# A selective-scan kernel with one more slot between its scans and what GpSimd and TensorE do with them

## The chip, the cores and the metric

The kernel runs on one core of one Trainium2 chip. The metric is the device time of one execution in microseconds. Before the change the median of three runs was 6442.46 us (6440.53 to 6453.84). Engines are called as in the profile: PE is TensorE's matmul, PEld its weight load, DVE is VectorE, ACT is ScalarE, POOL is GpSimd, and SP is the engine whose queue issues all DMAs of this kernel.

## The reference

Four layers work on `x` of shape (4, 96, 64, 64) in float32. The change touches the scan of layer 0 alone; layer 1 is a convolution block, layer 2 a spectral block with a small feed-forward network, layer 3 linear attention with another.

```python
# layer 0, for each of the 4 images; L = 4096, 192 channels d, 16 states n, 4 directions k
u     = silu(depthwise_conv(Win @ group_norm(x)))
xs    = [u, u^T, flip(u), flip(u^T)]                  # one sequence for each direction
dts, Bs, Cs = split(sel_w @ xs)
delta = softplus(dt_w @ dts + dt_b)
h     = h * exp(delta * A) + (delta * u) * B          # along L, for every (d, n)
y     = sum over n of h * C                           # + Ds * xs
out   = Wout @ layer_norm(y0 + y1 + y2 + y3)
```

So each of 4 images x 4 directions x 192 channels x 16 states is a recurrence over 4096 positions, followed by a product with C and a sum over the 16 states.

## The kernel before, in words

**Units and slots.** A sequence is cut into 8 chunks of 512 positions (`NCH`, `CH`). An image, a direction and a chunk make a *step*: 4 x 4 x 8 = 128 steps. A step is cut into 12 *units* (`u` = 0 to 11). A unit holds 64 channels (`i`) and 4 states (`j`) as two halves `e` of 128 partitions x 512 positions, so there are 1536 units. `PASSES` runs units 0 to 7 over `j` with `i` = 0 and 1 in turn, then units 8 to 11 over `j` with `i` = 2.

The loop at the end of `scans` has one *slot* for each unit. `manual_schedule` keeps every engine's instructions in the order in which this loop writes them; each engine, the DMA queue of SP too, works through its own list in order, and semaphores hold it where data or a buffer is missing. In slot s the loop writes, in this order:

- loads for the next step (`LOADS`, `fetch`) and the stores owed from the slot before (`flush`), both on SP;
- `decays(s + 1)`: on ACT, the two exponentials of the next unit into two PSUM banks `ps_da` (a ring of four banks, so two units). Before them `keep(s - 1)` copies the last column of the unit before into `state`, from which the next step's scan starts: two 128x1 copies on ACT, or one 128x2 copy on POOL where POOL makes the unit's product;
- `product(s - 1)`: on POOL, h times C, in place in the result tile `hc` (128x1024). Only the units of `POOL_C` have this, five of twelve;
- `inputs(s + 2)`: on POOL, the tile `db` = (delta u) B of the unit two slots ahead (128x1024), from a ring of three;
- `states(s)`: on DVE, two `tensor_tensor_scan` instructions. For the other seven units DVE also makes the two products with C, into `hc`;
- `sums`: on PE, for a pair of units, four matmuls with `const("stack")` into the single PSUM bank `ps_y`. The pair (s - 3, s - 2) is summed in slot s, since `when = at + 2` with `at` the odd unit. After the last pair of a pass ACT copies the bank to `yt`, and two stores to DRAM follow in the next slot;
- `advance`: work of all other layers, cut into small PE, ACT and DVE pieces (`Stage`), fills the slot up to a share of each engine. Its loads and stores go through the same SP queue.

**Buffers.** `SCAN` gives the rings: 3 tiles each for `rep_d` and `rep_g` (delta and delta u, repeated over partitions), 5 for `rep_BC` (rows of B and C, repeated), 3 for `db` and 5 for `hc`. A step uses four `rep_BC` tiles, `BC` 0 to 3, one for each `j`. A load into a tile waits until the last reader of its former content is done. `BC` 3 is loaded in slot 12 (`PC`), which is slot 0 of the step that uses it, and is first read by `inputs` of unit 6, in slot 4.

**Other work that hangs on the scans.** `through` counts finished steps in `scanned[b]`. The stages `turn` and `scan_outputs`, which add the four directions up, look at this count before they issue their loads. When the scans are over, the remaining stages of the last image are written without slots (`force`).

The lines of the profile: L1274 `inputs`, L1284 the exponentials, L1293 the scans, L1298 DVE's product with C, L1308 and L1310 the state copies, L1313 `product`, L1334 `sums`, L1345 the copy to `yt`, L1243 and L1249 the loads of `rep_BC` and of `rep_g` and `rep_d`, L444 the stores in `flush`.

Of the kernel before, what the change touches and what calls it, by code (L numbers as in the profile page):

```python
# [40 lines left out]

KORDER = [(0, 1, 3, 2)] * (B - 1) + [(1, 3, 0, 2)]

SCAN = {"rep_d": 3, "rep_g": 3, "rep_BC": 5, "db": 3, "hc": 5}
POOL_C = (1, 3, 6, 8, 10)
LAST = {"tab": 24, "more": 6}
TMP, IN = 10, 5

PC = NI * NJ // 2
# [46 lines left out]
def hybrid_kernel(ctx: ExitStack, tc: tile.TileContext, a: dict):  # L96
# [10 lines left out]
    pool = lambda name, bufs=1, **kw: ctx.enter_context(tc.tile_pool(name=name, bufs=bufs, **kw))  # L107
# [13 lines left out]
    def bank(tag="mm", turn=True):  # L121

        if alone and tag == "mm" and turn:
            tag = turns(alone)
        if tag == "mm":
            held_banks[0] += 1
        return psum.tile([128, CH], F32, name=f"ps_{tag}", tag=tag, bufs=BANKS[tag])
# [14 lines left out]
    def const(name, rows=slice(0, 128)):  # L142
        return cst[rows, CS[name]]
# [45 lines left out]
    def pair(tag):  # L189
        return sp.tile([128, 2, CH], F32, name=tag, tag=tag, bufs=SCAN[tag])  # L190

# [245 lines left out]
    def later(out, t, then=None):  # L437

        to_store.append((out, t, then))

    def flush():
        while to_store:
            out, t, then = to_store.pop(0)
            store(out, t)  # L444
            if then is not None:
                then()
# [753 lines left out]
    scanned = [0] * B  # L1200
# [15 lines left out]
    def scans(stages):  # L1216
# [12 lines left out]
        units = []  # L1229
        for number, step in enumerate(steps):  # L1230
            step["at"] = number % (K * NCH)
            u = 0
            for which, chans in enumerate(PASSES):
                for j in range(NJ):
                    for i in chans:
                        units.append({"step": step, "number": number, "u": u, "j": j, "i": i, "pass": which,
                                      "pool": u in POOL_C})
                        u += 1

        def load_states(step, j):  # L1240
            t = pair("rep_BC")
            of = d_bc[step["k"]][step["b"] % 3][step["c"], 8 * j : 8 * j + 8].rearrange("(s e) l -> s (e l)", e=2)
            load(t.rearrange("p e l -> p (e l)"), of.unsqueeze(0).to_broadcast([32, 4, 2 * CH]))  # L1243
            step["BC"][j] = t

        def load_channels(step, i, name):
            t = pair(f"rep_{name}")
            of = (d_delta if name == "d" else d_du)[step["k"]][step["b"] % 3][step["c"], 64 * i : 64 * i + 64]
            load(t.rearrange("p e l -> p (e l)"),  # L1249
                 of.rearrange("(p e) l -> p (e l)", e=2).unsqueeze(1).to_broadcast([32, 4, 2 * CH]))  # L1250
            step[name][i] = t

        def need(step):

            while (step["k"] % 2, step["c"]) not in traced[step["b"]]:
                force(stages)
            flush()


        LOADS = {4: [("BC", 0)], 5: [("g", 0)], 6: [("g", 1), ("d", 0)], 7: [("d", 1)], 10: [("BC", 1), ("g", 2)],  # L1260
                 11: [("BC", 2), ("d", 2)], PC: [("BC", 3)]}

        def fetch(step, what):
            for name, i in what:
                if name == "BC":
                    load_states(step, i)
                else:
                    load_channels(step, i, name)
# [3 lines left out]
        def inputs(x):  # L1272
            x["db"] = pair("db")
            nc.gpsimd.tensor_mul(x["db"], x["step"]["g"][x["i"]], both(x["step"]["BC"][x["j"]][:, 0]))  # L1274

        def decays(x, last):
            x["da"] = []
            for e in (0, 1):

                if last is not None:  # L1280
                    keep(last, e)
                av = (x["step"]["k"] * NI + 2 * x["i"] + e) * NJ + x["j"]
                x["da"].append(bank("da"))
                act(x["da"][e], x["step"]["d"][x["i"]][:, e], AF.Exp, scale=aneg[:, av : av + 1])  # L1284
# [15 lines left out]
        def keep(x, e):  # L1300
            step, u = x["step"], x["u"]
            if step["n"] < NCH - 1:
                if "last" not in step:
                    step["last"] = sp.tile([128, NI * NJ], F32, name="state")
                end = 0 if step["k"] >= 2 else CH - 1
                to = step["last"][:, 2 * u : 2 * u + 2]
                if not x["pool"]:
                    nc.scalar.copy(to[:, e : e + 1], x["h"][e][:, end : end + 1])  # L1308
                elif e == 0:
                    nc.gpsimd.tensor_copy(to, x["hc"][:, :, end])  # L1310

        def product(x):
            x["made"] = nc.gpsimd.tensor_mul(x["hc"], x["hc"], both(x["step"]["BC"][x["j"]][:, 1]))  # L1313

        due = {}
        for at in range(1, len(units), 2):
            group = units[at - 1 : at + 1]
            when = at + 2  # L1320
            due.setdefault(when, []).append(group)

        def sums(group):
            step, first, last = group[0]["step"], group[0]["j"] == 0, group[1]["j"] == NJ - 1
            if first:
                step["y"] = bank("y")
            y = step["y"]

            made = None
            for m in (1, 0):  # L1330
                x = group[m]
                for e in (1, 0):
                    q = 2 * m + e
                    done = mm(y[32 * q : 32 * q + 32], lhsT=const("stack"), rhs=x["hc"][:, e],  # L1334
                              start=first or (x["pass"] == 0 and x["j"] == 0), stop=last or (x["pass"] == 0 and x["j"] == NJ - 1))
                    if made is None:
                        made = group[0]["made"]
                        tc.add_manual_dep(done.ins, made.ins.name, mybir.DependencyInfo(
                            mybir.DependencyClass.Sync, mybir.DependencyReason.DATA), reason="sums")
            def through():  # L1340
                scanned[step["b"]] += 1

            if last:
                yt = sp.tile([128, CH], F32, name="yt")
                nc.scalar.copy(yt, y)  # L1345
                to = d_y[step["k"]][step["b"] % 2][step["c"]]
                for m in (0, 1):
                    at = 128 * group[0]["pass"] + 64 * m
                    later(to[at : at + 64].rearrange("(p e) l -> e p l", e=2), yt[64 * m : 64 * m + 64],
                          through if group[0]["pass"] == 1 and m == 1 else None)  # L1350

        owed = 0.0
        stages += plan()
# [5 lines left out]
        inputs(units[0])  # L1359
        inputs(units[1])  # L1360
        decays(units[0], None)
        for slot in range(len(units) + 6):
            clock[0] = slot
            x = units[slot] if slot < len(units) else None
            if x is not None:
                if x["u"] == 0:


                    last = len(units) - NCH * PC
                    if slot < last:  # L1370
                        rate = max(RATE, sum(s.work for s in stages if s not in behind) / (last - slot))
                    else:
                        rate = sum(s.work for s in stages) / (len(units) - slot)
                    if x["number"] > 0:
                        fetch(x["step"], LOADS[PC])
                if x["number"] + 1 < len(steps) and x["u"] in LOADS:
                    if x["u"] == 4:
                        need(steps[x["number"] + 1])
                    fetch(steps[x["number"] + 1], LOADS[x["u"]])
            flush()  # L1380
            if slot + 1 < len(units):
                decays(units[slot + 1], units[slot - 1] if slot > 0 else None)
            if 0 < slot <= len(units):
                if units[slot - 1]["pool"]:
                    product(units[slot - 1])
            if slot + 2 < len(units):
                inputs(units[slot + 2])
            if x is not None:
                states(x)
            for group in due.get(slot, ()):  # L1390
                sums(group)
            for e, (us, most) in SHARE.items():
                room[e] = min(room[e] + us, most)
            tensor[0] = 0.0
            held_banks[0] -= freed[0]
            freed[0] = 0
            owed = min(owed + rate, 8.0)
            while owed > 0.0:
                did = advance(stages)
                if did is None:  # L1400
                    break
                owed -= did
# [241 lines left out]
```

## Time and profile before

| what | value |
|---|---|
| median of 3 runs | 6442.46 us (6440.53 to 6453.84) |
| the profiled execution | 6432.73 us, of it 6430.9 us span on the core |
| granted TensorE clock, mean | 0.836 |
| busy: DVE | 5504.2 us (86%), 6059 instructions |
| busy: POOL | 5176.0 us (80%), 2743 instructions |
| busy: PE | 4759.6 us (74%), 27804 instructions |
| busy: ACT | 4172.2 us (65%), 8040 instructions |
| DMA | 1111.98 MB, 173 GB/s over the span |
| first scan begins, last scan ends | 89.6 us, 6015.9 us |
| mean length of a slot | 5926.3 us / 1536 = 3.86 us |

The durations and waits shown come from this one execution, which was 9.7 us shorter than the median. A busy share over the whole span mixes three parts: 90 us of preparation, 5926 us of slots, and 415 us after the last scan, in which POOL does nothing and PE is busy for 379.1 us. An engine's waits are read from the records of the instruction that starts after an idle time, with the semaphore that ended it.

### The profile page before, as it was taken

The page shows a single profiled execution, that of the slowest core. Times are in us where ns is not written, and L with a number is a line of the kernel's source. Part 1 is how long each engine was busy: PE and PEld are TensorE (multiplying, and loading weights), DVE is VectorE, ACT ScalarE, POOL GpSimd, SP SyncE. Part 2 cuts the span into 40 slices and gives each one's busy share as a digit, 9 for nine tenths or more (in the row PEclk, how much of TensorE's full clock was granted, in tenths as well). Part 3 has the DMA queues.
Part 4 walks back from the last instruction along what each step waited for, and adds up shares of the span by engine and source line. Part 5 has one row for each costly group of instructions (what it writes and reads, how often), then busy time and mean ns, then how long its engine had stood idle before and what let it go on. Part 6 is the DMA issues. An engine that isn't in the chain of part 4 may idle for free. (4 is left out here: it accounts for less than half of the span.)

```text
span 6430.9 us, 84514 instructions
## 1 busy us (share of the span) xinstructions
PE 4759.6 (74%) x27804; PEld 1744.9 (27%) x27804; DVE 5504.2 (86%) x6059; ACT 4172.2 (65%) x8040; POOL 5176.0 (80%) x2743
## 2 busy tenths in 40 slices
PE   7633867757987776786588877667987776857998
PEld 2100212111223621221122254211223531112374
DVE  5979998998999889999899998978999789898345
ACT  5743777865665677887466667856666577665435
POOL 4757878789999889987899988978999789899200
PEclk9755978878998877896799988888998787878999
DMA  5644565676544544466664455465644554555201
GB/s 190 207 155 140 192 208 189 203 236 230 190 152 162 175 164 150 159 201 209 238 216 162 149 183 180 153 215 186 183 155 157 176 173 168 197 189 177 96 10 41
DMA packets 434362, 1111.98 MB, mean 173 GB/s; under 512 B 72474, under 2 KB 74240, under 8 KB 432772
## 3 DMA queue, kind: packets, MB, share of 16 engines
q1 hardware_dynamic: 433924, 1106.58, 51.8%
q8 instruction: 221, 3.62, 0.2%
q14 instruction: 217, 1.78, 0.1%
HBM read 873.41 MB, written 237.44 MB: 173 GB/s over the span
## 5 line engine op out<-in xcount | busy, mean ns | idle before, releaser
L1274 POOL TENSOR_TENSOR db<-rep_g,rep_BC 128x1024 f32<-128x1024 f32 x1536 | 3597.5, 2364 | 344.3 <-DVE ps_da L1293 230.2
L1284 ACT ACTIVATE ps_da<-rep_d,aneg 128x512 f32<-128x512 f32 x3072 | 2062.5, 690 | 438.4 <-DVE hc L1293 320.8
L1293 DVE TENSOR_TENSOR_SCAN ps_da<-ps_da,state,db 128x512 f32<-128x512 f32 x1568 | 1923.2, 1271 | 312.5 <-ACT state L1308 201.3
L1313 POOL TENSOR_TENSOR hc<-hc,rep_BC 128x1024 f32<-128x1024 f32 x640 | 1511.8, 2362 | 112.5 <-DVE hc L1293 58.8
L1334 PE MATMUL ps_y<-hc,cst 128*32 128x512 f32 x6144 | 1018.5, 741 | 627.4 <-POOL hc L1313 352.1
L1293 DVE TENSOR_TENSOR_SCAN hc<-ps_da,state,db 128x512 f32<-128x512 f32 x1120 | 1370.9, 1265 | 107.2 <-issue 43.9
L1298 DVE TENSOR_TENSOR hc<-ps_da,rep_BC 128x512 f32<-128x512 f32 x1792 | 1134.5, 674 | 0.1
L1308 ACT COPY state<-ps_da 128x1 f32<-128x1 f32 x1568 | 247.1, 158 | 499.0 <-DVE hc L1298 498.0
L1334 PEld LDWEIGHTS ps_y<-hc,cst 128*32 128x32 f32 x6144 | 144.7, 118 | 1265.4 <-POOL hc L1313 735.2
L1310 POOL COPY state<-hc 128x2 f32<-128x2 f32 x560 | 106.1, 189 | 369.3 <-DVE hc L1293 341.7
L818 PE MATMUL ps_mm<-h,wd 128*32 128x512 f32 x3192 | 367.1, 595 | 8.3 <-ACT r L155 8.3
L552 PE MATMUL ps_mm<-xp,taps 128*128 128x512 f32 x576 | 295.3, 655 | 52.3 <-ACT ua L554 20.6
L1293 DVE TENSOR_TENSOR_SCAN ps_da<-ps_da,db 128x512 f32<-128x512 f32 x224 | 261.1, 1210 | 51.0 <-ACT state L1308 29.5
L795 PE MATMUL ps_mm<-wd,w 128*32 128x512 f32 x2016 | 256.2, 624 | 32.2 <-DMA wd<-x 20.2
L1345 ACT COPY yt<-ps_y 128x512 f32<-128x512 f32 x256 | 149.2, 583 | 165.1 <-PE ps_y L1334 163.2
L603 PE MATMUL ps_mm<-xd,dtw 128*128 128x512 f32 x256 | 167.0, 745 | 98.4 <-ACT z L625 52.4
L877 PE MATMUL ps_mm<-r,cst 128*128 128x512 f32 x214 | 148.5, 783 | 62.8 <-ACT r L874 18.2
L1293 DVE TENSOR_TENSOR_SCAN hc<-ps_da,db 128x512 f32<-128x512 f32 x160 | 186.0, 1202 | 6.8 <-POOL db L1274 3.0
L799 ACT ACTIVATE h<-ps_mm 128x512 f32<-128x512 f32 x265 | 152.9, 598 | 58.9 <-PE ps_mm L795 57.1
L990 PE MATMUL ps_mm<-wa,xp 128*64 128x96 f32 x1728 | 136.8, 319 | 72.5 <-DVE d L995 61.1
L618 DVE SCALAR_TENSOR_TENSOR ps_mm<-ps_mm,z 128x512 f32<-128x512 f32 x192 | 131.6, 686 | 58.1 <-ACT z L616 54.8
L552 PEld LDWEIGHTS ps_mm<-xp,taps 128*128 128x128 f32 x576 | 115.1, 207 | 228.7 <-issue 159.5
(341 smaller groups left out, 6802.4 us busy)
## 6 DMA issues: line engine op xcount, KB each, us to landing
rep_BC<-bc SPq DMA_DIRECT2D x512, 512.0 KB
rep_g<-du SPq DMA_DIRECT2D x384, 512.0 KB
rep_d<-delta SPq DMA_DIRECT2D x384, 512.0 KB
y<-yt SPq DMA_DIRECT2D x512, 128.0 KB
du<-g SPq DMA_DIRECT2D x128, 256.0 KB
delta<-z SPq DMA_DIRECT2D x128, 256.0 KB
tab<-in_etab SPq DMA_DIRECT2D x112, 256.0 KB
ypart<-y SPq DMA_DIRECT2D x72, 256.0 KB
```

The costliest lines, as they stand in the source:

```text
L552: mm(p, lhsT=taps[:, t, 0:128], rhs=window(t, c + e), start=t == 0, stop=t == 8)
L603: mm(p, lhsT=dtw[:, o + 2 * part, 0:128], rhs=xd, start=True, stop=True)
L795: mm(p[32 * n : 32 * n + 32], lhsT=w1[:, 32 * g : 32 * g + 32], rhs=xin[:, n : n + 15 : 2, 1 : W + 1], start=True, stop=True)
L799: act(h[:, :, 1 : W + 1], split(p), AF.Relu)
L818: mm(p[32 * n : 32 * n + 32], lhsT=held["wd"][:, groups[i], o, dx, :], rhs=here[i][:, :, dx : dx + W], start=dx == 0, stop=dx == 2)
L1274: nc.gpsimd.tensor_mul(x["db"], x["step"]["g"][x["i"]], both(x["step"]["BC"][x["j"]][:, 0]))
L1284: act(x["da"][e], x["step"]["d"][x["i"]][:, e], AF.Exp, scale=aneg[:, av : av + 1])
L1293: nc.vector.tensor_tensor_scan(x["h"][e][:, order], x["da"][e][:, order], x["db"][:, e, order], start, ALU.mult, ALU.add)
L1298: x["made"] = nc.vector.tensor_mul(x["hc"][:, e], x["h"][e], x["step"]["BC"][x["j"]][:, 1])
L1308: nc.scalar.copy(to[:, e : e + 1], x["h"][e][:, end : end + 1])
L1313: x["made"] = nc.gpsimd.tensor_mul(x["hc"], x["hc"], both(x["step"]["BC"][x["j"]][:, 1]))
L1334: done = mm(y[32 * q : 32 * q + 32], lhsT=const("stack"), rhs=x["hc"][:, e], start=first or (x["pass"] == 0 and x["j"] == 0), stop=last or ...
```

## The change

It moves three things later by whole slots, changes two rings and the set of units that POOL multiplies.

- `product` is written for unit s - 2 instead of s - 1, and after `inputs(s + 2)` instead of ahead of it. The state copy of POOL's units moves with it, out of `decays` into `product`.
- `sums` of a pair come two slots later (`at + 4`). The copy to `yt` and its two stores no longer follow the matmuls directly: `sums_out` writes the copy in the slot after, behind that slot's exponentials. `through` is then called with the later stores.
- `db` has 4 tiles instead of 3, `hc` 7 instead of 5.
- `POOL_C` is (1, 3, 5, 7, 10) instead of (1, 3, 6, 8, 10): still five of twelve.
- `BC` 3 is loaded in slot 13, which is slot 1 of its own step.

The number of instructions on PE, DVE, ACT and POOL stays the same; their order changes.

```diff
-SCAN = {"rep_d": 3, "rep_g": 3, "rep_BC": 5, "db": 3, "hc": 5}
-POOL_C = (1, 3, 6, 8, 10)
+SCAN = {"rep_d": 3, "rep_g": 3, "rep_BC": 5, "db": 4, "hc": 7}
+POOL_C = (1, 3, 5, 7, 10)
...
-                 11: [("BC", 2), ("d", 2)], PC: [("BC", 3)]}
+                 11: [("BC", 2), ("d", 2)], PC + 1: [("BC", 3)]}
...
-                if last is not None:
+                if last is not None and not last["pool"]:
                     keep(last, e)
...
         def product(x):
+            keep(x, 0)
             x["made"] = nc.gpsimd.tensor_mul(x["hc"], x["hc"], both(x["step"]["BC"][x["j"]][:, 1]))
...
-        due = {}
+        def through(b):
+            scanned[b] += 1
+
+        due, summed = {}, []
         for at in range(1, len(units), 2):
             group = units[at - 1 : at + 1]
-            when = at + 2
+            when = at + 4
             due.setdefault(when, []).append(group)
...
             if last:
+                summed.append((group, y))
+
+        def sums_out():
+            while summed:
+                group, y = summed.pop(0)
+                step = group[0]["step"]
                 yt = sp.tile([128, CH], F32, name="yt")
                 nc.scalar.copy(yt, y)
...
-                    if x["number"] > 0:
-                        fetch(x["step"], LOADS[PC])
+                if x["number"] > 0 and PC + x["u"] in LOADS:
+                    fetch(x["step"], LOADS[PC + x["u"]])
...
             if slot + 1 < len(units):
                 decays(units[slot + 1], units[slot - 1] if slot > 0 else None)
-            if 0 < slot <= len(units):
-                if units[slot - 1]["pool"]:
-                    product(units[slot - 1])
+            sums_out()
             if slot + 2 < len(units):
                 inputs(units[slot + 2])
+            if 2 <= slot < len(units) + 2 and units[slot - 2]["pool"]:
+                product(units[slot - 2])
             if x is not None:
                 states(x)
```

More of the change, by code (lines that the diff above doesn't have):

```diff
@@ L1339, in sums @@
                             mybir.DependencyClass.Sync, mybir.DependencyReason.DATA), reason="sums")
-            def through():
-                scanned[step["b"]] += 1
             if last:
+                summed.append((group, y))
[3 more added lines that the diff above has]
+                step = group[0]["step"]
                 yt = sp.tile([128, CH], F32, name="yt")
@@ L1349, in sums @@
                     later(to[at : at + 64].rearrange("(p e) l -> e p l", e=2), yt[64 * m : 64 * m + 64],
-                          through if group[0]["pass"] == 1 and m == 1 else None)
+                          (lambda b=step["b"]: through(b)) if group[0]["pass"] == 1 and m == 1 else None)
         owed = 0.0
```

## Prediction

> **What bounds the kernel now.** I first read the page's busy shares and its costliest groups.
>
> ```profile
> PE 4759.6 (74%) x27804; PEld 1744.9 (27%) x27804; DVE 5504.2 (86%) x6059; ACT 4172.2 (65%) x8040; POOL 5176.0 (80%) x2743
> ...
> L1274 POOL TENSOR_TENSOR db<-rep_g,rep_BC 128x1024 f32<-128x1024 f32 x1536 | 3597.5, 2364 | 344.3 <-DVE ps_da L1293 230.2
> L1293 DVE TENSOR_TENSOR_SCAN ps_da<-ps_da,state,db 128x512 f32<-128x512 f32 x1568 | 1923.2, 1271 | 312.5 <-ACT state L1308 201.3
> L1313 POOL TENSOR_TENSOR hc<-hc,rep_BC 128x1024 f32<-128x1024 f32 x640 | 1511.8, 2362 | 112.5 <-DVE hc L1293 58.8
> L1298 DVE TENSOR_TENSOR hc<-ps_da,rep_BC 128x512 f32<-128x512 f32 x1792 | 1134.5, 674 | 0.1
> ```
>
> DVE and POOL lead, but neither is full. The windows view (length; then busy us and instructions of PE, PEld, DVE, ACT, POOL; clock; DMA) shows this for the slots:
>
> ```profile
> 1500.00:3000.00 1500.00, 1159.26 (x6931) 426.76 (x6929) 1371.11 (x1474) 1060.31 (x2055) 1349.74 (x716) 0.84 0.52 175
> 3000.00:4500.00 1500.00, 1133.22 (x6751) 405.86 (x6750) 1333.02 (x1424) 973.75 (x1918) 1344.40 (x714) 0.85 0.56 188
> ```
>
> With the outer windows, DVE is busy 5315 us and POOL 5158 us of the 5926 us of slots: DVE idles 611 us, POOL 768 us. The waits of POOL and DVE over that stretch tell who holds whom:
>
> ```profile
> POOL state L1310 <- DVE hc L1293: 341.7, 215, 6.1
> POOL db L1274 <- DVE ps_da L1293: 230.2, 112, 43.4
> POOL hc L1313 <- DVE hc L1293: 58.8, 35, 3.9
> ```
>
> ```profile
> DVE ps_da L1293 <- ACT state L1308: 230.9, 119, 8.5
> DVE ps_da L1293 <- POOL db L1274: 61.3, 59, 8.8
> DVE ps_da L1293 <- ACT ps_da L1284: 57.7, 39, 6.4
> DVE hc L1293 <- POOL db L1274: 26.3, 15, 4.0
> ```
>
> POOL waits 631 us for DVE; DVE waits 88 us for POOL and far more for ACT. So DVE paces the slots, and POOL's large idle time is worth only what comes back to DVE. I then paired each scan record, in order, with its exponential (two for a unit) and its `db`, and put the idle time before it down to whichever ended later. Of 474 us before scans, ACT was last for 417 us (240 scans) and POOL for 57 us (54). Of the latter 2.6 us would stay with POOL in time.
>
> Why is ACT late? Followed back on ACT to its last idle time, nearly every case is a wait for PE. The largest single line is the copy to `yt` (31 scans, 62 us). Following PE back to its last idle time over 0.3 us, 79 scans (211 us) start at a stage matmul that waited for a load, some 12 us earlier. SP works its list in order, so its waits delay those loads:
>
> ```profile
> SPq L1249 <- POOL db L1274: 1052.8, 336, 13.2
> SPq L1243 <- POOL hc L1313: 757.6, 172, 15.0
> SPq L444 <- ACT yt L1345: 370.6, 74, 18.2
> ```
>
> **What the skill says.** The Trainium skill, SBUF — State Buffer, section "SBUF: two separate sides", says that DVE and GpSimd exclude each other only where the DVE operation is in a two-port mode or has two SBUF inputs. Here DVE's scan and its product with C each read one of their two tensors from `ps_da` in PSUM, and the trace agrees: a scan has a median of 1266 ns with POOL busy throughout and 1262 ns with POOL idle, a product 674 and 676. A denser POOL should not stretch DVE. Perfetto Trace Analysis, section "Optimization Strategy", says that a gap which repeats on the engine that should be full can mean too few buffers for the next tile. The POOL waits above fit: `db` cannot be written until the scan three units back has freed its tile. DMA: Bandwidth & Descriptors, "Issuing engines are not separate DMA queues", has all DMAs share the same 16 engines; they are 51.8% occupied by packets here, so I take order on SP, not bandwidth, as what delays loads.
>
> **The change part by part.** Everything is counted against the profiled 6432.7 us, 9.7 us under the median.
>
> *Order on POOL, ring `db`.* Nothing is added: 1536 `db` products, 640 products with C and their 560 state copies (189 ns) stay. Before, slot s on POOL needed the scans of s - 1 finished and had then, within two slots (7.7 us), up to 0.19 + 2.36 + 2.36 = 4.9 us to do before scan s + 2. After, it needs only scans s - 2: the same 4.9 us in three slots, 11.6 us. The median `db` was ready 3.4 us before its scan, and one in twenty 0.04 us; both gain up to a slot, 3.86 us. POOL's work is 5158 / 1536 = 3.36 us a slot, so it can keep that lead. Gain: 57 - 3 = **54 us**, at most the 88 us of the waits view, at least 30 if POOL lags in the denser slots. The new `POOL_C` moves two products by a slot and adds none.
>
> *The copy to `yt`.* 256 copies of 583 ns on ACT move from behind their matmuls to behind the next slot's exponentials. ACT waited 163 us at them (76 times); behind it stand the stage's ACT work and the next exponentials, for which DVE waits. Of the 62 us that this cost DVE I take two thirds, **41 us**: where PE is far behind, the next stage operation on ACT waits for the same PE. Bounds: 0 and 62.
>
> *Sums two slots later.* 768 groups pass two slots of stage matmuls on PE. PE's waits there for POOL (352 us) should go. I cost this at nothing: PE's last idle time before a late ACT was a `ps_y` wait on POOL in only 6 of 240 cases (7 us). `hc`: a unit takes the tile of seven units before, summed two or three slots earlier, as with five tiles before, so DVE is not held more than now (15.6 us, twice).
>
> *SP.* Loads of `rep_g` wait for POOL's `db` products, which now run up to a slot earlier. `BC` 1 (slot 10) takes the tile last read by unit 8, now a DVE product in slot 8, instead of POOL's in slot 9. `BC` 3 (127 loads) goes in slot 13 and waits for POOL's product of unit 10, now in slot 12 behind a `db`; the 512 stores of `yt` come three slots later, still a slot behind their copy. Net, SP should stand half a slot ahead of before, bounded by the stores that wait for ACT. The 79 scans lose 2.7 us each on average; loads that come 1 to 2 us earlier save between 0 and half of the 211 us. I take a quarter, **53 us**.
>
> *The ends.* The built programs have the same instruction counts, and 2102 instead of 2086 matmul records after the last sum; the tail of 415 us stays, -5 to +10 us, taken as 0.
>
> Sum: 54 + 41 + 53 = 148 us. When DVE arrives earlier, ACT and PE have less time per slot. PE's row of slices shows 8 or more in 9 of the 37 slices with scans, and ACT's lateness is 88% of the idle time before scans; between these I let a third come back as ACT waits, an estimate. 148 x 2/3 = 99, and 6432.7 - 99 = 6333.7: **6335 us**, with its own range 6265 to 6405 (bounds of the three terms).
>
> **Rivals.**
>
> *More than that.* SP's lead is worth half its 211 us and little comes back: (54 + 62 + 105) x 0.9 = 199, so 6234 us. For it speaks how much of ACT's lateness begins at loads; against it, that those loads also wait for their own tiles.
>
> *ACT and PE are the pacer.* The 54 and 41 us return as ACT waits, since ACT was last for 417 of 474 us: 6410 to 6445 us. Against it: in the 54 POOL-late scans ACT alone would have cost only 2.6 us.
>
> *`BC` 3 arrives too late: slower.* Place: `inputs` of unit 6 in slot 4, once in each of 127 steps. From issue to that first read the trace has a median of 17.0 us. After, the load is issued a slot later (3.86), its tile is freed behind one more `db` and a state copy (2.55), and POOL reads a slot earlier (3.86): 6.7 us are left to POOL. DVE is reached only when POOL's lead, 3.4 + 3.86 = 7.2 us, is used up too: at 13.9 us. Each us beyond costs 127 us, and from 13.9 + 99/127 = 14.7 us on the kernel is slower. At 15.4 us it would take 6432.7 - 99 + 190 = 6524 us. Against it: `BC` 1 has only 9.5 us (median; 7.5 least), and POOL waited for it once after the first step. For it: SP is at times over 10 us behind its slot, and POOL did wait for row loads seven times in the slots, up to 9.3 us.
>
> **How the numbers follow.** About 0.2% (13 us) is what a measurement of this kernel tells from no change. Forecast case 0.48; more 0.13; pacer 0.20 (0.09 of it faster, 0.08 within 0.2%, 0.03 slower); `BC` 3 or a like stall 0.19. So faster 0.70, same 0.08, slower 0.22. The range 6225 to 6460 takes in most of the second case, the third, and the start of the fourth, and leaves out about 0.05 below and 0.14 above.
>
> **What would show it.** Right: POOL's waits on DVE fall from 631 us to below 250; DVE's on POOL from 88 to below 20; ACT's on `ps_y` from 163 to below 40; DVE idle in the slots near 510 us with about 5315 us busy; slots of 3.79 us. SP's wait for POOL at L1249 falls by a third or more. Wrong: DVE's waits on ACT grow from 307 us by what the POOL waits lose (pacer), or POOL waits at `db` for `rep_BC` in slot 4 of most steps and DVE waits for POOL (`BC` 3), or DVE's scan grows over 1271 ns.

## The result and the profile after

The changed kernel takes 6400.8 us (median of 5 runs, 6395.8 to 6409.8) against 6442.5 us (5 runs): a ratio of 0.994, 95% interval 0.9927 to 0.9954, so 41.7 us or 0.65% faster. In a second set on another occasion it was 0.9947 (0.9929 to 0.9964). The profiled execution was the slowest of the five, 6409.8 us with a span of 6408.0 us, while the one of before had been 9.7 us under its median. The two traces therefore differ by 22.9 us only. Counted from the first instruction, the slots run from 78.5 to 6004.8 us before and from 78.6 to 5976.2 us after: 28.7 us shorter. The tail, which is the time after the last scan, grew from 426.2 to 431.8 us. (The two times of scans in the table ahead count from 11.1 us earlier. The windows of the prediction were laid between them and so lie 11 us late: the tail of 415 us named there is this one of 426, and its 5315 us busy and 611 us idle for DVE are 5325 and 601 us over the slots themselves.)

The costliest groups of the profile, in the order line, operation, count, busy us, mean ns, idle time before and its main cause:

```profile
L1274 POOL TENSOR_TENSOR db<-rep_g,rep_BC 128x1024 f32<-128x1024 f32 x1536 | 3608.6, 2365 | 753.4 <-DVE hc L1293 352.1
L1293 DVE TENSOR_TENSOR_SCAN ps_da<-ps_da,state,db 128x512 f32<-128x512 f32 x1568 | 1922.4, 1271 | 284.8 <-ACT state L1308 166.3
L1314 POOL TENSOR_TENSOR hc<-hc,rep_BC 128x1024 f32<-128x1024 f32 x640 | 1511.0, 2361 | 48.5 <-DVE hc L1293 3.7
L1298 DVE TENSOR_TENSOR hc<-ps_da,rep_BC 128x512 f32<-128x512 f32 x1792 | 1133.7, 673 | 0.2
```

None of these four durations moved. POOL's waits have gone from the products to the `db` line. Each line below gives an engine and its line, what ended its wait, the total in us, how often, and the longest. The waits of POOL in the slots come first, then of DVE, then of PE, with PE's of the kernel before; SP's wait at the load L1249 ends the list:

```profile
POOL db L1274 <- DVE hc L1293: 352.1, 209, 3.9
POOL db L1274 <- DVE ps_da L1293: 161.2, 85, 38.2
POOL db L1274 <- DMA rep_BC<-bc: 131.3, 30, 13.3
```

```profile
DVE ps_da L1293 <- ACT state L1308: 180.7, 102, 9.5
DVE ps_da L1293 <- ACT ps_da L1284: 92.0, 48, 7.5
DVE hc L1293 <- ACT ps_da L1284: 34.6, 18, 3.6
DVE ps_da L1293 <- POOL db L1274: 21.6, 22, 2.8
DVE hc L1293 <- POOL db L1274: 14.0, 12, 3.1
```

```profile
PE ps_y L1338 <- POOL hc L1314: 215.6, 72, 8.4
PE ps_y L1338 <- ACT yt L1352: 207.3, 54, 19.6
PE ps_y L1334 <- POOL hc L1313: 352.1, 93, 49.3
```

```profile
SPq L1249 <- POOL db L1274: 533.5, 102, 12.2
```

DVE waits less for POOL (88 us to 36 us at `db`, with 17 us of new waits at POOL's product and state copy) and slightly more for ACT (307 us to 325 us, with 17.5 us at a line not shown). PE has a wait that was 2.6 us before: for the single bank `ps_y`, until ACT has copied it. Paired as in the prediction (each scan with its exponential and its `db`), DVE's idle time before scans goes from 474 to 469 us: POOL last falls from 57 to 26 us, ACT last goes from 417 to 438 us. One profile can move ACT's number by as much: ring_only, below, takes the time of the kernel before and shows 439.

DVE is idle for 589 us of the slots instead of 601, and busy for 5308 us instead of 5325. So in this pair of traces more than half of the 28.7 us is not in waits at all. Of the 17 us, 11 are two lines of stage work, L905 (65.6 to 59.7 us in the slots) and L1126 (11.3 to 5.8 us). Over the whole execution, before and then after:

```profile
L905 DVE TENSOR_SCALAR acc<-acc,bq 128x512 f16<-128x512 f16 x96 | 81.3, 857 | 14.2 <-ACT acc L900 14.0
L905 DVE TENSOR_SCALAR acc<-acc,bq 128x512 f16<-128x512 f16 x96 | 75.4, 796 | 16.9 <-ACT acc L900 16.7
```

In the kernel before, L905 took 349 ns on average where POOL was idle (49 times, all but one in the tail) and 1531 ns where POOL worked throughout (26 times). The 38 that took over 600 ns in the slots ended a median of 0.15 us after a POOL operation did. So they are held until POOL's operation is over, and what they cost depends on where they fall. A second profile of the changed kernel has 579 us idle, 5311 us busy and 59.0 us at L905.

### The profile page after: what moved, and what is told of

It is laid out like the page before. It is cut to its first block, busy times and chain, and to the rows that moved or that the text cites. A ratio compares the mean times of both kernels' runs of the same rounds, so it can differ in the third digit from the quotient of the medians.

```text
span 6408.0 us, 84715 instructions
## 1 busy us (share of the span) xinstructions
PE 4763.2 (74%) x27804; PEld 1766.1 (28%) x27804; DVE 5488.4 (86%) x6059; ACT 4178.6 (65%) x8040; POOL 5171.1 (81%) x2743
## 5 line engine op out<-in xcount | busy, mean ns | idle before, releaser
L1293 DVE TENSOR_TENSOR_SCAN hc<-ps_da,state,db 128x512 f32<-128x512 f32 x1120 | 1370.8, 1264 | 135.2 <-issue 41.7
L1338 PE MATMUL ps_y<-hc,cst 128*32 128x512 f32 x6144 | 1004.1, 732 | 524.2 <-POOL hc L1314 215.6
L1293 DVE TENSOR_TENSOR_SCAN hc<-ps_da,db 128x512 f32<-128x512 f32 x160 | 186.1, 1203 | 22.9 <-issue 16.4
L705 PE MATMUL ps_mm<-ypart,cst 128*128 128x512 f32 (+1 forms) x272 | 158.0, 704 | 38.1 <-DMA ypart<-yt 37.4
L612 ACT ACTIVATE z<-ps_mm 128x512 f32<-128x512 f32 x192 | 114.2, 595 | 96.6 <-PE ps_mm L603 48.2
```

Of the source, the lines that this page charges most:

```text
L705: mm(p, lhsT=const(name, slice(0, s.shape[0])), rhs=s, start=n == 0, stop=n == len(of) - 1)
L1293: nc.vector.tensor_tensor_scan(x["h"][e][:, order], x["da"][e][:, order], x["db"][:, e, order], start, ALU.mult, ALU.add)
```

## The experiments

All ratios are to the kernel before, run beside it; intervals are 95%. In the edits, "..." marks code left out, and short lines stand side by side.

**Where the copy stands.** With the copy directly behind its matmuls in the changed kernel, and with the late copy alone in the kernel before:

```diff
# copy_at_once (from the changed kernel)
-            sums_out()
             if slot + 2 < len(units):
...
             for group in due.get(slot, ()):
                 sums(group)
+            sums_out()
# copy_later (from the kernel before), sums still at + 2
             if last:
-                yt = sp.tile([128, CH], F32, name="yt")
-                nc.scalar.copy(yt, y)
...
+                summed.append((group, y))
...
+            sums_out()
             if 0 < slot <= len(units):
```

> The changed kernel, with the copy to yt put back directly behind its matmuls (same slot); sums still two slots later. Backlog theory: the copy was only the first ACT operation to meet a late PE, so its place is worth nothing: 6400 us within 10, and ACT again waits at the copy (some 100 us) while its other waits for PE shrink by as much. Copy theory (the prediction's term of 41 us, with a third coming back): 6400 + 27 = 6427 us. Tie theory: the copy a slot later makes PE wait 207 us for the single bank ps_y, which delays the stages; then at once is better, 6380 us or less.

> The kernel before, with the copy to yt (and its stores) one slot later and nothing else. Backlog theory: no change, 6442 within 10 us; ACT's 163 us at the copy go, and its waits for PE at stage lines grow by as much. Copy theory: 6442 - 27 = 6415 us. Tie theory: slower than before, 6450 us or more, with PE waiting for the copy.

copy_at_once took 6385.7 us, 0.9918 (0.9905 to 0.9931). That rules out the copy theory's 6427 us and lies between the other two (6390 to 6410, and 6380 or less). copy_later took 6416.3 us, 0.9972 (0.9961 to 0.9983), the figure of the copy theory (6415): beside early sums the late copy gains 18 us (within 11 to 25). Its trace does not show this as less lateness. ACT last is 423 us (417 before), DVE idles 611 us of the slots (601 before), and ACT's waits have moved to another line that needs PE, L669 (first before, then copy_later):

```profile
ACT yt L1345 <- PE ps_y L1334: 163.2, 76, 9.8
ACT yrow L669 <- PE ps_mm L665: 104.0, 37, 8.1
ACT yrow L669 <- PE ps_mm L665: 139.9, 42, 9.5
```

What its trace does show is DVE busy 18 us less, with 23 us less at L905 and L1126. So the gain of copy_later is measured, but that it comes from ACT's wait is not shown.

Beside late sums the late copy gains nothing: the kernel without it is the faster one by 14 us (19 against the second set), though the intervals overlap a little. The waits of PE and ACT in copy_at_once:

```profile
PE ps_y L1338 <- ACT yt L1352: 71.6, 16, 10.7
ACT yt L1352 <- PE ps_y L1338: 170.1, 80, 9.6
ACT yrow L669 <- PE ps_mm L665: 112.7, 40, 8.0
```

and the same two of ACT in the changed kernel:

```profile
ACT yrow L669 <- PE ps_mm L665: 153.4, 46, 14.6
ACT yt L1352 <- PE ps_y L1338: 5.9, 2, 3.2
```

ACT's wait at the copy does go, from 170 to 6 us, and part of it is back at L669. PE pays with the bank: 207 instead of 72 us. Against that stand 80 us less wait for POOL at the same line. PE's idle time before these matmuls as a whole, first of copy_at_once, then of the changed kernel, grows by 96 us:

```profile
L1338 PE MATMUL ps_y<-hc,cst 128*32 128x512 f32 x6144 | 1005.0, 733 | 427.9 <-POOL hc L1314 296.0
L1338 PE MATMUL ps_y<-hc,cst 128*32 128x512 f32 x6144 | 1004.1, 732 | 524.2 <-POOL hc L1314 215.6
```

That the bank is what costs the 14 us fits but was not isolated; a second `ps_y` bank was not tried, since the kernel has given out all the banks it holds (`BANKS`: 3, 4 and 1).

**POOL's part, the sums, the ring and the units, one by one.**

```diff
# ring_only
-"db": 3, "hc": 5}
+"db": 4, "hc": 5}
# sums_later
-"db": 3, "hc": 5}          when = at + 2
+"db": 3, "hc": 7}          when = at + 4
# pool_order
-"db": 3, "hc": 5}          PC: [("BC", 3)]
+"db": 4, "hc": 5}          PC + 1: [("BC", 3)]
...
-            if 0 < slot <= len(units):
-                if units[slot - 1]["pool"]:
-                    product(units[slot - 1])
             if slot + 2 < len(units):
                 inputs(units[slot + 2])
+            if 2 <= slot < len(units) + 2 and units[slot - 2]["pool"]:
+                product(units[slot - 2])
# pool_and_sums: as pool_order, and
-"db": 4, "hc": 5}          when = at + 2
+"db": 4, "hc": 7}          when = at + 4
# units_only
-POOL_C = (1, 3, 6, 8, 10)
+POOL_C = (1, 3, 5, 7, 10)
```

> The kernel before with four db tiles instead of three and nothing else. Theory that the order on POOL (product ahead of inputs, for the unit just scanned) holds POOL: no change, 6438 within 10 us, DVE scans for which db is last stay near 57 us. Theory that the ring holds it: those fall below 30 us and the time is 6415 us or less.

> The kernel before, with sums two slots later and seven hc tiles, copy directly behind them, nothing else. POOL theory: no change, 6442 within 10 us, though PE's wait for POOL's products at ps_y falls below 150 us. If those waits of PE were what made ACT late, ACT's share of the idle time before scans falls from 417 us by 50 or more and the time is about 6400 us.

> The kernel before, with POOL's part alone: db ring of four, product and state copy a slot later and behind inputs, BC 3 loaded a slot later. Sums, copy, hc ring and POOL_C as before. POOL theory (all of the gain comes from POOL's earlier db products): about 6442 - 31 = 6411 us, DVE scans for which db is last fall from 57 us to below 30. If the sums have to move with the products: PE waits for POOL's product in every group (over 352 us) and the time is 6440 us or more.

> The kernel before with POOL's part (db ring of four, product and state copy a slot later, BC 3 a slot later) and with the sums two slots later (seven hc tiles); the copy directly behind its matmuls and POOL_C (1, 3, 6, 8, 10) as before. It differs from copy_at_once by POOL_C alone. Theory that POOL's part pays once PE no longer waits for the products: the 978 us of PE at ps_y in pool_order fall below 350 and the time is 6440 - 45 = 6395 us or less. If the new POOL_C carries the gain (BC 1's tile is free earlier): 6425 us or more.

> The kernel before with POOL_C (1, 3, 5, 7, 10) and nothing else. Theory that POOL_C only repairs the load of BC 1 under the later products: within 10 us of the kernel before, 6440. Theory that it is worth something by itself: 6400 us or less.

| kernel | median us | ratio (interval) | db last, us | ACT last, us |
|---|---|---|---|---|
| ring_only | 6446.4 | 1.0005 (0.9995 to 1.0014) | 55 | 439 |
| sums_later | 6428.4 | 0.9986 (0.9977 to 0.9995) | 56 | 418 |
| pool_order | 6695.1 | 1.0401 (1.0387 to 1.0414) | 33 | 636 |
| pool_and_sums | 6494.7 | 1.0075 (1.0059 to 1.0090) | 61 | 479 |
| units_only | 6421.3 | 0.9974 (0.9965 to 0.9984) | 66 | 396 |
| copy_at_once: pool_and_sums with the new units | 6385.7 | 0.9918 (0.9905 to 0.9931) | 38 | 416 |

The two right-hand columns are the pairing above. A fourth `db` tile alone does nothing, so the repeated wait at `db` was no sign of too few tiles by itself: POOL was held by its order, product ahead of `inputs`. The new order alone costs 257 us. The sums of a pair now stand in the slot of POOL's product and PE waits for it, with the stages and then ACT behind. In pool_order:

```profile
PE ps_y L1335 <- POOL hc L1314: 978.7, 259, 46.8
```

With the sums two slots later and seven `hc` tiles, in pool_and_sums, that falls to 281 us, and 200 of the 257 us are gone:

```profile
PE ps_y L1335 <- POOL hc L1314: 281.2, 84, 15.9
```

But pool_and_sums is still slower than the kernel before. SP's waits, first of pool_and_sums, then of copy_at_once, which differs by `POOL_C` alone:

```profile
SPq L1243 <- POOL hc L1314: 1181.6, 168, 17.4
```

```profile
SPq L1243 <- DVE hc L1298: 479.9, 123, 15.0
SPq L1243 <- POOL hc L1314: 139.3, 54, 6.6
```

`BC` 1 is loaded in slot 10 into the tile of `BC` 0, whose last reader is the product of unit 8. With POOL's product moved into slot 10, SP stands still until POOL gets there: before the loads of `BC` 1 alone it stood 1064 us, against 406 us in copy_at_once. `BC` 1 went out 1.6 us after the scan of its slot began (median), and POOL read it after only 4.1 us, having waited for it:

```profile
POOL db L1274 <- DMA rep_BC<-bc: 309.0, 132, 39.9
```

With unit 8 on DVE, `BC` 1 goes out 3.4 us ahead of that scan. The new units are worth 17 us by themselves (units_only) and about 100 us under the new order (1.0075 - 0.9918 of 6440). PE's wait for POOL at `ps_y` is no rival for this, as it is much the same in both (281 and 296 us). That all of the 100 us comes by way of `BC` 1 is read from the traces; a sixth `rep_BC` tile under the old units was not tried.

**Later places for ACT's work, deeper loads, a sixth row tile.** These ask whether the ACT waits that remain can be had back. The first two change `fits`, which decides whether ACT may take a stage's result in the slot of its matmuls: only while the slot has had at most so many us of stage matmuls. The deeper loads ask for a stage's tables and rows one item earlier.

```diff
# evict_later (from the changed kernel; evict_mid with 1.5)
-            if (was, engine) != ("pe", "act") or tensor[0] > 1.9:
+            if (was, engine) != ("pe", "act") or tensor[0] > 1.0:
# before_deep, after_deep
-            return ahead(2, table, range(n))
+            return ahead(3, table, range(n))
...
-            chunks = ahead(1, fetch, range(NCH))
+            chunks = ahead(2, fetch, range(NCH))
# at_once_deep: after_deep and copy_at_once together
# bc_six (from copy_at_once)
-"rep_BC": 5, "db": 4, "hc": 7}          when = at + 4
+"rep_BC": 6, "db": 4, "hc": 6}          when = at + 3
```

> The changed kernel; the planner lets ACT take a stage's result in the slot of its matmuls only while that slot has had up to 1.0 us of stage matmuls, instead of 1.9. Theory that ACT is late because PE's own work of a slot is not done when ACT asks for it: ACT's share of the idle time before scans (438 us) falls by 80 or more and the time is 6360 us or less. Theory that PE is behind by more than a slot, so a later place doesn't help, or that held banks slow the stages: 6400 us within 10, or more.

> The changed kernel with the bound for ACT's same-slot work at 1.5 us of stage matmuls instead of 1.9 (evict_later had 1.0). Price theory: the slots get shorter than 5890 us by some 100 us and the tail longer than 432 us by as much or more, 6400 to 6450 us in all. Loss theory: the tail stays below 480 us and the time is 6350 us or less.

evict_later: 6502.0 us, 1.0100 (1.0084 to 1.0116). ACT last falls from 438 to 233 us and the slots shrink from 5898 to 5680 us, but the tail grows from 432 to 739 us. evict_mid: 6511.9 us, 1.0117 (1.0099 to 1.0134), slots 5812, tail 616 us. The windows of evict_later (slots, then tail), and those of the changed kernel below them, show where it went: 5004 instead of 4002 weight loads are left for the tail.

```profile
79.00:5759.00 5680.00, 4034.68 (x22632) 1377.08 (x22634) 5274.41 (x5686) 3856.92 (x7493) 5154.19 (x2735) 0.82 0.56 185
5759.00:6498.00 739.00, 683.86 (x5012) 315.66 (x5004) 213.97 (x409) 273.93 (x443) 0.53 (x1) 0.97 0.22 65
79.00:5976.00 5897.00, 4315.66 (x23676) 1516.93 (x23676) 5307.72 (x5727) 3974.65 (x7722) 5159.49 (x2735) 0.82 0.56 183
5976.00:6408.00 432.00, 398.44 (x4010) 228.96 (x4002) 165.74 (x304) 175.29 (x277) 0.00 (x0) 0.98 0.14 44
```

So some 200 us of ACT's lateness can be had away, but not for nothing. About 1000 matmuls and 33 us of DVE's work left the slots with it, so how much of the shorter slots is saved waiting and how much is work moved out is not separated. With `fits` as it is, the waits are, at least in part, the price of having the stages done inside the slots. Both expectations of a gain failed, and the price theory was too mild: the time lost in the tail is more than that won in the slots.

> The kernel before, with the stages' loads asked for one item earlier: tables three ahead instead of two, rows of turn two ahead instead of one. Theory that ACT is late because PE's stage matmuls wait for loads that SP issues late (211 us of DVE's idle time start there): these fall by half or more, and the time is 6438 - 70 = 6370 us. Theory that SP's queue, not the depth, is what makes them late (a load asked for earlier only stands in the same blocked queue), or that another wait takes over: 6438 within 15 us.

> The changed kernel with the same deeper loads of the stages as before_deep. Load theory: ACT's waits at L669, L1041 and its copies of the spectral stage, 160 us of DVE's idle time, fall by half and the time is 6400 - 60 = 6340 us. Otherwise 6400 within 15 us.

> The changed kernel with the copy to yt directly behind its matmuls and the stages' loads one item deeper. If the place of the copy is worth 15 us also here (copy_at_once against the changed kernel) and the deeper loads their 26 us: 6441 x 0.9875 = 6361 us. If the two do the same thing (PE earlier at the stages): as after_deep, 6378 us.

before_deep: 6420.1 us, 0.9963 (0.9951 to 0.9975). after_deep: 6377.7 us, 0.9900 (0.9885 to 0.9914). at_once_deep: 6369.6 us, 0.9895 (0.9876 to 0.9913). Deeper loads gain 0.4% beside either kernel, well under half of what the load theory asked for. In before_deep the lateness that begins at a load fell from 211 to 189 us and not by half. at_once_deep has the lowest median of all kernels run and beats both kernels of this case; on this base the place of the copy makes no measurable difference to after_deep.

> The changed kernel with the copy at once, six rep_BC tiles, six hc tiles and sums one slot later instead of two. A row's tile is then free long before its load. Theory that the rows' loads take what is left of POOL's lateness: POOL's waits for rep_BC fall from 154 us to below 40, DVE scans for which db is last from 38 us to below 15, and the time is 6385 - 20 = 6365 us. Otherwise 6385 us within 10.

bc_six: 6384.1 us, 0.9925 (0.9906 to 0.9944), the same as copy_at_once. The scans for which `db` is last fell from 38 to 14 us, and nothing came of it. It is no clean test of POOL's lateness: the sums, a slot earlier with six `hc` tiles, made PE wait 464 us for POOL instead of 296, and POOL's waits for `rep_BC` fell from 154 to 90 us only, not below 40.

> The changed kernel once more, to stand beside the others of this set on one chip. 0.994 of the kernel before, within 0.0015.

after_again: 6404.3 us, 0.9947 (0.9929 to 0.9964); its pairing gives 24 us for POOL and 431 us for ACT.

## Why the prediction was wrong

The direction was right, and in part by luck: without the new `POOL_C`, which was costed at nothing, the new order and the later sums make a slower kernel (pool_and_sums, by 0.75%). The size was not right: 99 us were forecast from the profiled execution, 42 us came in the medians. 6400.8 us lies inside the whole range and the forecast case's own (6265 to 6405). All three terms were to come as less idle time of DVE before scans. That fell by 5 us in the first pair of traces and by 16 us in the second, and 15 to 17 us more came from DVE's work, chiefly L905 and L1126, for which no term stood.

- **Order on POOL (54 us).** The mechanism was right and the size was off: scans for which `db` is last fell by 31 us. "Both gain up to a slot" is the step that was too large. The median `db` is now ready 7.4 us before its scan instead of 3.4, a whole slot (3.86 us) more; but one in twenty has 0.7 us instead of 0.04, and those are the ones that DVE waits for. The ring alone gave nothing and the order needed two companions. The prediction said that `POOL_C` "moves two products by a slot and adds none" and costed it at nothing. That was the largest omission: under the new order it decides 100 us, most likely through the load of `BC` 1. The paragraph on SP had named that tile, and counted only half a slot for all of SP's lead.
- **The copy to `yt` (41 us).** This term failed. ACT's wait at the copy fell from 163 to 6 us, as foreseen, but ACT's lateness as a whole did not fall: 438 us, and 431 in the second trace, against 417. Followed back as in the prediction, the 62 us that began at the copy are gone, and those that begin at two other ACT operations that wait for PE, L669 and the copy behind L1063, went from 56 to 108 us. The copy had mostly been the first operation to meet a late PE. The caveat was in the text, a third of the 62 us; here it took nearly all. The time of copy_later, 18 us better with early sums, speaks for a gain there, but its trace does not show one at ACT; and late sums make PE wait for the bank.
- **SP (53 us).** This term failed too. SP did move ahead: `BC` 1 went out 3.4 us ahead of its slot's scan instead of 0.9, `BC` 2 went from 0.7 us behind to 2.1 us ahead (means), and SP's wait for POOL at L1249 fell from 1053 to 534 us. Yet the ACT lateness that I had traced to loads went from 211 to 206 us only. The step that failed is the one from SP's lead to PE. PE's own waits for loads in the slots were 113 us in 35 cases before, less than the 211 us, and they did not fall with SP ahead: 156 us in 36 cases. So "PE's last idle time ended at a load" marks where PE's busy stretch began, some 12 us earlier, and does not say how much of its lateness at the end is the load's. Asking for the loads earlier recovered 21 us in the kernel before. Why PE's waits for loads grew is open.
- **Sums, counted at nothing.** By themselves nearly right: 0.9986. But PE's wait there for POOL did not go, as the prediction had it; it fell from 352 to 216 us, since POOL's product moved later as well (with the product in its old place, in sums_later, it is 42). And the sums are what makes POOL's order possible, about 200 us between pool_order and pool_and_sums.
- **A third comes back.** Too little: of the 31 us that POOL freed, 5 us stayed in the first trace, and 16 of 33 in the second. bc_six took 24 us of POOL's lateness away for no gain, with the other changes named above.
- **The ends.** Taken as 0, +6 us measured (+10 in the second profile), inside the stated bounds.
- **Two slips in the sum.** The upper end of the case's own range takes the lower bound of 30 us whole; with a third coming back it would be 6413 us. And in the profile of the kernel before, PE's row of slices shows 8 or more in 10 of the 37, not 9. Neither changes the account.
- **Signs foreseen.** POOL's waits on DVE were to fall below 250 us; they are 517 us. POOL is still faster than the slots, so it waits for DVE at another line. ACT on `ps_y` below 40 us: right. DVE on POOL below 20 us: 36 us at `db`. DVE idle near 510 us: 589 us. Slots of 3.79 us: 3.84. SP at L1249 down by a third: right.
- **The rivals.** *More than that* did not come: SP's lead gave next to nothing. *ACT and PE are the pacer* describes the rest in part: ACT's lateness stayed. Its own figures, 6410 to 6445 us, were too high. *`BC` 3 too late* did not happen; 10.4 us were left from issue to first read instead of 6.7, and a load needs about 4.

## What to carry to other kernels

When a step is moved by a slot, look at each buffer that it is the last to read, and at what stands in the loading queue behind the load that takes that buffer: here the choice of the unit that is read last decided 100 us, more than the slack that the move was made for. Before a wait is priced as gain, ask whether the waiting engine's next instruction needs the same late producer; if so, the wait can move to that instruction, and little is won. Going back to the last idle time of a producer shows when its backlog began, not what caused it.

## What the runs showed of the hardware

The time from the issue of a 512 KB row load to its use was shorter than I had bounded it. Where POOL was waiting for `BC` 1 (pool_and_sums), the first read began 4.1 us after the issue (median, 3.6 at the least), while in the kernel before 7.5 us was the least ever left to `BC` 1. The kernel before had already shown a `BC` 2 that was read 4.3 us after its issue, with POOL waiting for it.

A scan or a product on DVE takes the same whether POOL works or not: in the changed kernel a scan has a median of 1265 ns with POOL busy throughout and 1261 ns with POOL idle, a product 673 ns in both. The prediction had looked at these alone. Other DVE operations do not go free: L905, a `tensor_scalar` on 128x512 f16, took 349 ns with POOL idle and 1531 ns with POOL busy (means, kernel before), and its long cases ended 0.15 us after the POOL operation beside them. In the slots of all traces together, the 25 that met no POOL operation took 322 to 355 ns.
